# Quarter products that accumulate in shared PSUM tiles, a bias add moved to GpSimd, and a new bank split at the end of attention

## The chip, the cores and the metric

The kernel runs on one core of a Trainium2 chip. The metric is device time in microseconds (us), lower is better. The time before is 655.55 us, the median of three runs (655.39 to 655.63). One more execution was taken with the hardware profiler; all durations below are from that one.

## The reference

One decoder layer over x (2 batches x 512 tokens x 1024) and a context (2 x 1024 x 1024), all in float32:

```python
x = x + attention(layernorm(x), w_qkv, b_qkv, w_o, b_o)     # 32 heads of 32, 8 key/value heads, RoPE, causal
x = x + fake_quant(layernorm(x)) @ fake_quant(ctx)          # 512x1024 @ 1024x1024 for each batch
x = x + ffn(layernorm(x))                                   # below
# fake_quant(v) = (clip(round(v / s + z), 0, 255) - z) * s
# ffn(x): base  = x @ W_org.T
#         coeff = softmax((mean over tokens of x) @ Wq.T @ keys.T / sqrt(128))      # 8 experts
#         delta = sum over e of coeff[e] * (x @ down[e]) @ up[e]                     # rank 64 each
#         return base + delta
```

## The kernel before

**Stages.** Batch 0 and batch 1 are called 0 and 1. First come layer norm, the q, k and v products and the rotation. Then attention runs in 40 slots, followed by visits that only finish earlier slots. In the slots, PE also gets "fill": the second half of the k, q and v products, and batch 0's output product, context product and layer norms. After attention comes the tail: batch 1's output product ("wo"), batch 1's context product, the W_org product for both batches ("wb"), the low-rank "hidden" product, and the "up" product, which ends the kernel.

**An order written out by a planner.** The order of instructions on PE, DVE (VectorE), ACT (ScalarE) and Pool (GpSimd) is fixed when the program is built. `Clocks` estimates what each engine's clock would read after each instruction. Work off PE waits in `lanes` as `Hop`s; `dispatch` emits the head of a lane, in the sorted order of lane names, while its engine's estimated clock is at most `LEAD` (0.6 us) ahead of PE's, and `force(key)` emits lanes until that key is done. In the tail, units of PE work come from `g_post`, and at a `yield PAUSE` inside a long unit the small units whose inputs are ready (context tokens `C`, transposes `X`, column sums `cs`) are put between. Bulk loads are issued on SP's (SyncE's) queue; the bias row `bo`, the transposing DMAs of `mT` and `q1T` on ACT's.

**PSUM banks.** There are eight banks of 128x512, in two sets of four. `mm` takes a free bank among `allowed`, the one read longest ago. In attention a visit `i` computes scores into one set (`new`) and the transposed scores of slot `i - LAG` ("weights", L1218 and L1226) into the other (`old`). ACT turns weights into `pt` with an exponential (L1240), Pool masks `pt`'s diagonal blocks (L1245), `attend` multiplies `pt` by the values (L1267), and `evacuate` copies the result into `oT`. After each visit `allowed` is the set that fill may use, and the sets change roles (`filler`).

**Products by quarters.** Five products (wo of batch 1, wb of both batches, hidden, up) use Winograd's form of Strassen's scheme (`by_quarters`). Each matrix is cut in quarters, and seven products of quarter size take the place of eight:

```
P1 = A11 B11     P2 = A12 B21     P3 = S4 B22     P4 = A22 T4
P5 = S1 T1       P6 = S2 T2       P7 = S3 T3
C11 = P1 + P2                     C12 = P1 + P6 + P5 + P3
C21 = P1 + P6 + P7 + P4           C22 = P1 + P6 + P5 + P7
```

S and T are sums of quarters that DVE makes: `left_sums` and the tiles `s_`; `right_sums`, whose four groups are the keys ("to", 0) to ("to", 3) for wo, "tb" for wb, "td" for hidden and "tu" for up. The code counts quarters from 0, so that C12 is `(0, 1)`. In the row products each quarter product fills two banks with four matmuls each, in the up product four banks with two each; a matmul of two float32 operands is two instructions in the profile. Every product takes banks of its own. DVE adds a finished bank into the rows of `x` (`add`, L1795 and L1866) or into `hs` (L1835); hidden's first add of a quarter is a scaled copy on ACT. P1 is also copied by ACT into an SBUF tile `more` (L1724); DVE then adds P6 and later P7 into it (`gather`, L1711), and `more` goes into the quarters of C. The order is 2, 1, 5, 6, 3, 7, 4, in the up product 2, 1, 5, 6, 7, 3, 4. For wo of batch 1, P2 is computed while attention ends (`beside`).

**The other parts that the change touches.** `bias_lane` adds b_o to the four row tiles of x (128x1024 each) on DVE (L1046). `load_ctx` quantises the context in eight chunks; in the tail Pool sums their columns one chunk after another into `q2sum` (L1382), and `g_columns` turns that into column totals on PE with a matrix of ones (L1390). `quantize_rows` makes the bf16 rows `a1` and issues their transposing DMA (L1510), which sets the key ("A", b, t).

Of the kernel before, what the change touches and what calls it, by code (L numbers as in the profile page):

```python
# [111 lines left out]
class Clocks:  # L112
# [45 lines left out]
    def add(self, ins):  # L158
# [34 lines left out]
        elif engine == "PE":  # L193
            wide = "float32" in str(ins_[0].dtype)
            passes = 1 if not wide else 2 if ins.is_transpose else 4
            size = tuple(ins.tile_size) if ins.tile_size else (128, 128)
            if size != self.tile_size:
                start = max([start] + self.groups) + 0.2
                self.tile_size = size
            whole = size[0] * size[1] == 16384  # L200
            part = range(4) if whole else [max(ins.tile_position) // 32]
            done = max([start] + [self.groups[i] for i in part]) + max(n * passes / 2400.0, 0.055)
            for i in part:
                self.groups[i] = done
            self.at[engine] = done if whole else start + 0.015
            end = done + 0.2
        else:
            many = max([n] + [_free(a) for a in ins_])
            if kind in self.FIXED:
                us = self.FIXED[kind]  # L210
            elif many <= 16:
                us = self.SMALL
            elif engine == "Activation":
                scaled = len(ins_) > 1 and len(outs) == 1
                us = 0.15 + 0.00084 * many + 0.12 * (len(outs) > 1 or scaled and many > 900)
            elif engine == "Pool":
                us = 0.25 + 0.0008 * many
            elif kind == "CustomDveAnt":
                us = 0.08 + 0.00104 * many
            elif kind == "TensorScalarPtr" and len(ins_) < 2 + 2 and not ins.is_scalar_tensor_tensor:  # L220
                us = 0.12 + 0.00058 * many
            else:
                us = 0.08 + 0.00106 * many
                if kind == "TensorScalarPtr":
                    us += 0.05
                elif kind == "TensorTensor" and self.at["Pool"] > start and not _in_psum(ins_):
                    us += 0.1
            if kind == "TensorTensor" and engine == "Pool" and many <= 16:
                us = 0.45
            self.at[engine] = start + us  # L230
            end = start + us + 0.08
# [15 lines left out]
def kernel(  # L247
# [142 lines left out]
    taken = {}  # L390

# [34 lines left out]
    def mm(shape, name, dtype=F32):  # L426

        clocks.catch_up()
        could = [p for p in allowed if is_free(p)]
# [69 lines left out]
    LEAD = 0.6  # L499
    LEADS = {"Activation": 5.0, "Pool": 5.0}  # L500
# [117 lines left out]
    def fill(us):  # L618

        credit[0] += us  # L620
        while any_may() and (is_open() or credit[0] > UNIT / 2):
            if not step():
                credit[0] = min(credit[0], UNIT)
                break
# [420 lines left out]
    def add_bo(xi, bo_sb):  # L1045
        nc.vector.tensor_tensor(xi, xi, bo_sb, ALU.add)  # L1046

    def bias_lane(b, x_tiles, load):
# [16 lines left out]
        for t in range(NT):  # L1065
            lane(
                (4, "bias"),
                Hop("DVE", lambda t=t: add(t), lambda t=t: [got[0], x_tiles[t]], key=("bias", b, t), us=1.2),
# [206 lines left out]
    def attended_to(g, pv):  # L1275

        b, c = divmod(g, NC)
        if b not in oT:
            oT[b] = act.tile([P, NC, S], F32, tag="act", name=f"oT{b}")
        evacuate(oT[b][:, c, :], pv)  # L1280
# [6 lines left out]
    def load_ctx(b, bufs, dst, release):  # L1287
# [72 lines left out]
        if free[0]:  # L1360
            for k in range(1, CTX // P):
                mine = [("q2", b, i) for i, (n_, _) in enumerate(parts) if n_ in (k - 1, k)]
                last = {"key": ("q2sum", b), "made": lambda: [q2sum[b]]} if k == CTX // P - 1 else {}
# [20 lines left out]
    def g_columns(b):  # L1384
        corr[b] = const.tile([P, D], F32, tag="corr", name=f"corr{b}")
        for h in range(2):
            cols = slice(h * 512, (h + 1) * 512)
            ps = mm([P, 512], f"cs{b}_{h}")
            if b in q2sum:
                nc.tensor.matmul(ps, onesh, q2sum[b][:, cols], start=True, stop=True)  # L1390
# [303 lines left out]
    def by_quarters(product, a_, b_, s_, t_, more, add, hooks=(), late_third=False, ps2=None):  # L1694
# [8 lines left out]
        banks = range(len(more))  # L1703

        def add_all(i, j, srcs, first=False):
            for h in banks:
                add(i, j, h, srcs[h], first)

        def gather(ps):
            for h in banks:  # L1710
                nc.vector.tensor_tensor(more[h], more[h], ps[h], ALU.add)  # L1711

        if ps2:
            add_all(0, 0, ps2, True)
            then(0)
        else:
            then(0)
            ps = yield from product(2, a_(0, 1), b_(1, 0))
            add_all(0, 0, ps, True)
        then(2)  # L1720
        yield PAUSE
        ps = yield from product(1, a_(0, 0), b_(0, 0))
        for h in banks:
            nc.scalar.copy(more[h], ps[h])  # L1724
        add_all(0, 0, ps)
        then(1)
        yield PAUSE
        ps = yield from product(5, s_[0], t_(1))
        minus_(s_[0], a_(0, 1), s_[1])
        add_all(0, 1, ps, True)  # L1730
        add_all(1, 1, ps, True)
        then(5)
        yield PAUSE
        ps = yield from product(6, s_[1], t_(2))
        if len(s_) == 2:
            minus_(s_[1], a_(0, 0), a_(1, 0))
        gather(ps)
        add_all(0, 1, more)
        then(6)
        yield PAUSE  # L1740

        def third():
            ps = yield from product(3, s_[0], b_(1, 1))
            add_all(0, 1, ps)
            then(3)
            yield PAUSE

        def seventh():
            ps = yield from product(7, s_[-1], b_(0, 1))
            gather(ps)  # L1750
            add_all(1, 1, more)
            add_all(1, 0, more, True)
            then(7)
            yield PAUSE

        for p in (seventh, third) if late_third else (third, seventh):
            yield from p()
        ps = yield from product(4, a_(1, 1), t_(4))
        add_all(1, 0, ps)
        then(4)  # L1760

    def left_sums(s_, a_):
        nc.vector.tensor_tensor(s_[0], a_(1, 0), a_(1, 1), ALU.add)
        minus_(s_[1], s_[0], a_(0, 0))
        if len(s_) == 3:
            minus_(s_[2], a_(0, 0), a_(1, 0))

    def rows_product(name, b, pauses=True):
        def product(p, l, r):
            n = NK // 2  # L1770
            ps = [mm([P, 512], f"{name}{p}_{b}_{i}") for i in range(2)]
            for i in range(2):
                for k in range(n):
                    nc.tensor.matmul(  # L1774
                        ps[i], l[:, k, i * P : (i + 1) * P], r(k), start=(k == 0), stop=(k == n - 1)
                    )
                    yield 0.86
                if not i and pauses:
# [5 lines left out]
    def rows_by_quarters(name, b, lhs, weight, t_, hooks, ps2=None):  # L1784
# [13 lines left out]
        more = tail["more"]([P, 2, 512], f"more{name}{b}")  # L1798
        if not ps2:
            hooks[0] = [lambda: left_sums(s_, a_)] + hooks.get(0, [])  # L1800
        yield from by_quarters(product, a_, b_, s_, t_, [more[:, i, :] for i in range(2)], add, hooks, ps2=ps2)
# [3 lines left out]
    def store(b, t, cols):  # L1805
        i = b * NT + t
        nc.sync.dma_start(out[i * P : (i + 1) * P, cols], xs[b][t][:, cols])

    def hidden_by_quarters():
# [7 lines left out]
        def product(p, l, r):  # L1817
            ps = [mm([P, S], f"h{p}_{i}") for i in range(2)]
            for i in range(2):
                for k in range(n):  # L1820
                    nc.tensor.matmul(  # L1821
                        ps[i], r(k)[:, i * P : (i + 1) * P], l[:, k, :], start=(k == 0), stop=(k == n - 1)
                    )
                    yield 0.86
            return ps
# [12 lines left out]
        s_ = [act.tile([P, n, S], F32, tag="half", name=f"sh{i}") for i in range(2)]  # L1838
        more = tail["more"]([P, 2, S], "moreh")
        left_sums(s_, a_)  # L1840
# [3 lines left out]
        yield from by_quarters(product, a_, b_, s_, t_, [more[:, i, :] for i in range(2)], add)  # L1844

    def up_by_quarters():
# [6 lines left out]
        def product(p, l, r):  # L1853
            ps = [mm([P, 512], f"up{p}_{t}") for t in tiles]
            for t in tiles:
                for k in range(n):
                    nc.tensor.matmul(  # L1857
                        ps[t], l[:, k, t * P : (t + 1) * P], r(k), start=(k == 0), stop=(k == n - 1)
                    )
                    yield 0.86  # L1860
            return ps
# [9 lines left out]
        parts = {(0, 0): 2, (0, 1): 3, (1, 0): 2, (1, 1): 2}  # L1871
# [3 lines left out]
        more = [tail["q2"]([P, 2, S], f"moreu{i}") for i in range(2)]  # L1875
        more = [m[:, i, :] for m in more for i in range(2)]

        def sums_left():
            left_sums(s_, a_)

        def sums_right():
# [3 lines left out]

        yield from by_quarters(
            product, a_, b_, s_, t_, more, add, {0: [sums_right], 2: [sums_left]}, True
        )

    def chain_units(b, w_keys):  # L1890

        turned = [("q", n) for n in range(B * NC)] + [("k", n, h) for n in range(B) for h in range(2)]
        columns = [("q2sum", b)] if b else [("q2", b, i) for i in range(CTX // P)]
# [146 lines left out]
    def visit(i):  # L2040
# [29 lines left out]
        for s in range(4):  # L2070
            if s == 1 and g >= 0:
                empty([(new, 0)])
                pv = take_bank((new, 0))
# [16 lines left out]
        filler[0] = new  # L2090
        last_slots = i + 1 >= n_slots
        allowed[:] = [(1 - new if last_slots else new, s) for s in range(4)]
# [57 lines left out]

    def output_left(i):
        s_ = [sums["S"][:, j, :, :] for j in range(2)]
        a_ = lambda i, j: oT[1][:, (1 - j) * half : (2 - j) * half, i * 256 : (i + 1) * 256]
        if i:
# [4 lines left out]
    def sums_lane(makers, name, sources):  # L2159

        for i, fns in enumerate(makers):
            for k, fn in enumerate(fns):
                key = {"key": (name, i)} if k == len(fns) - 1 else {}
                lane((1 if name == "to" else 2, name), Hop("DVE", fn, lambda k=k: sources(k), **key))
# [5 lines left out]
    )  # L2170
    sums_lane(wo_makers, "to", lambda k: ())
# [26 lines left out]
    def output_by_quarters():  # L2198
# [3 lines left out]
            2: [lambda: force(("S1",)), lambda: force(("to", 0))],  # L2202
            5: [lambda: force(("to", 1))],
            3: [lambda: rows_quantised(0), lambda: force(("to", 2)), lambda: org_rows(0)],
# [5 lines left out]
    def base_unit(b):  # L2210
        hooks = {}
        if b == 0:
# [5 lines left out]
                1: [lambda: force(("tb", 0))],  # L2218
                5: [lambda: force(("tb", 1))],
                3: [lambda: force(("tb", 2))],  # L2220
                7: [lambda: force(("tb", 3))],
            }
        yield from rows_by_quarters("wb", b, x3T[b], lambda k: org[k], org_sums[0], hooks)
# [94 lines left out]
```

## Time and profile before

| | us |
|---|---|
| median of the three runs | 655.55 |
| the profiled execution's own time | 655.19 |
| its span, first to last instruction | 653.5 |
| PE busy | 631.9 (97%) |
| DVE busy | 514.5 (79%) |
| ACT busy | 299.6 (46%) |
| Pool busy | 128.8 (20%) |
| granted TensorE clock, mean | 0.999 |

The span is what a profile's rows cover, and 1.7 us of the execution's time lie outside it. PE is busy almost throughout, so most rows of the profile describe work beside PE's. Rows of the timeline have the start, the duration, the engine, the line, the operation, what it writes and reads, shapes and a count, and in brackets the idle time of the engine before it with what ended that. Rows of the list of waits have the waiting engine and line, who released it, the total, the number and the longest. PEld is PE's weight load; an engine's name with a q is its queue, SPq for example.

### The profile page before, as it was taken

The numbers are of one execution on the slowest core, as the hardware profiler recorded it, in microseconds if no ns is written. First come the engines' busy times: TensorE is split into PE (matmuls) and PEld (weight loads), VectorE is DVE, ScalarE is ACT, GpSimd is POOL, SyncE is SP. The second block draws the span as 40 slices with busy tenths as digits, with TensorE's granted clock in tenths as the row PEclk, the third lists the DMA queues.
The fourth block names the chain that finished last, engine by engine and source line by source line (L and its number), as shares of the span: only waits on it lengthen the run. The fifth ranks groups of instructions, "written<-read, shape, count | busy, mean of one in ns | idle before, by whom it ended". The sixth has DMA issues, their size and how long they took to land. (4 is left out here: it accounts for less than half of the span.)

```text
span 653.5 us, 9247 instructions
## 1 busy us (share of the span) xinstructions
PE 631.9 (97%) x3190; PEld 301.6 (46%) x3190; DVE 514.5 (79%) x1187; ACT 299.6 (46%) x808; POOL 128.8 (20%) x253
## 2 busy tenths in 40 slices
PE   5998999999999999999999999999999999999997
PEld 5753344444444444444444444444345544444443
DVE  5799889888778988888887689998998544553685
ACT  2145576686655768888897433554101100110100
POOL 2100133233313232333233320440110000000000
PEclk9999999999999999999999999999999999999999
DMA  9930000002021230120101146591000002000105
GB/s 290 335 83 2 9 9 10 10 1 73 10 73 65 73 106 10 46 101 34 33 2 25 25 134 237 169 314 32 1 1 0 33 31 97 1 0 1 65 0 193
DMA packets 42478, 44.64 MB, mean 68 GB/s; under 512 B 19264, under 2 KB 32576, under 8 KB 42432
## 3 DMA queue, kind: packets, MB, share of 16 engines
q1 hardware_dynamic: 24992, 38.82, 17.4%
q10 hardware_dynamic: 17440, 5.25, 4.2%
q8 instruction: 25, 0.41, 0.2%
q14 instruction: 21, 0.17, 0.1%
HBM read 35.66 MB, written 4.19 MB: 61 GB/s over the span
## 5 line engine op out<-in xcount | busy, mean ns | idle before, releaser
L1147 ACT ACTIVATE ms<-ms,stats 128x512 f32<-128x512 f32 (+3 forms) x256 | 141.0, 558 | 70.1 <-DVE stats L1132 70.1
L1132 DVE CUSTOM_DVE_ANT_0 ms<-bank,mask 128x512 f32<-128x512 f32 (+3 forms) x256 | 108.5, 487 | 14.7 <-PE bank L1120 12.9
L1240 ACT ACTIVATE pt<-bank 128x512 f32<-128x512 f32 x160 | 88.0, 590 | 25.3 <-PE bank L1267 9.0
L751 PE MATMUL bank<-xT,wq 128*128 128x512 f32 x192 | 88.0, 600 | 2.7 <-DVE stats L1132 2.7
L1245 POOL TENSOR_SCALAR_AFFINE_SELECT pt<-pt 128x512 f32<-128x512 f32 x64 | 48.9, 782 | 94.5 <-ACT pt L1240 90.3
L1411 PE MATMUL bank<-wo,oT 128*128 128x512 f32 x128 | 59.1, 604 | 0.7 <-ACT pt L1240 0.7
L751 PEld LDWEIGHTS bank<-xT,wq 128*128 128x128 f32 x192 | 34.7, 190 | 41.3 <-issue 35.7
L1218 PE MATMUL bank<-qT,kT 32*128 32x128 f32 (+3 forms) x512 | 49.3, 439 | 1.3 <-DVE x L1420 0.6
L1147 ACT ACTIVATION_READ_ACCUMULATOR ms<-ms,stats 128x1 f32 x256 | 50.1, 196 | 0.0
L1120 PE MATMUL bank<-kT,qT 32*128 32x128 f32 (+3 forms) x512 | 49.0, 461 | 0.0
L1120 PEld LDWEIGHTS bank<-kT,qT 32*128 32x128 f32 x512 | 24.2, 183 | 34.9 <-ACT pt L1240 10.5
L1267 PE MATMUL bank<-pt,v 128*32 128x128 f32 (+3 forms) x512 | 37.8, 435 | 0.0
L1411 PEld LDWEIGHTS bank<-wo,oT 128*128 128x128 f32 x128 | 23.1, 189 | 26.8 <-issue 24.2
L1193 POOL TENSOR_TENSOR stats<-stats,log 128x16 f32<-128x16 f32 x16 | 6.5, 409 | 142.7 <-ACT log L1184 100.3
L1218 PEld LDWEIGHTS bank<-qT,kT 32*128 32x128 f32 x512 | 25.6, 185 | 14.6 <-issue 7.8
L1795 DVE TENSOR_TENSOR x<-x,bank 128x512 f32<-128x512 f32 x36 | 23.1, 680 | 11.1 <-PE bank L1774 5.7
L1411 PE MATMUL bank<-q,q1T 128*128 128x512 bf16 x128 | 28.6, 379 | 1.6 <-ACT pt L1240 1.6
L1267 PEld LDWEIGHTS bank<-pt,v 128*32 128x32 f32 x512 | 16.4, 109 | 27.7 <-issue 24.8
L1774 PE MATMUL bank<-worg,S 128*128 128x512 f32 x64 | 28.3, 592 | 0.0
L1774 PE MATMUL bank<-worg,x3T 128*128 128x512 f32 x64 | 28.0, 594 | 0.0
L1774 PE MATMUL bank<-tb,S 128*128 128x512 f32 x64 | 27.9, 593 | 0.0
L743 DVE TENSOR_TENSOR qT<-bank,qT 128x512 f32<-128x512 f32 x28 | 18.9, 686 | 9.6 <-PE bank L751 9.5
(226 smaller groups left out, 1021.4 us busy)
## 6 DMA issues: line engine op xcount, KB each, us to landing
wq<-in_wqT_dram SPq DMA_DIRECT2D x8, 512.0 KB, 8.5
ctx_raw<-in_ctx_dram SPq DMA_DIRECT2D x8, 512.0 KB, 3.2
wo<-in_woT_dram SPq DMA_DIRECT2D x8, 512.0 KB, 3.1
raw<-in_ctx_dram SPq DMA_DIRECT2D x8, 512.0 KB, 3.9
worg<-in_worgT_dram SPq DMA_DIRECT2D x8, 512.0 KB, 6.2
out_dram<-x SPq DMA_DIRECT2D x16, 256.0 KB, 2.1
x<-in_x_dram SPq DMA_DIRECT2D x7, 512.0 KB, 6.7
x_raw<-in_x_dram SPq DMA_DIRECT2D x4, 512.0 KB, 7.4
```

What stands on the lines that cost most here:

```text
L743: nc.vector.tensor_tensor(dst, ps, other, ALU.add)
L751: nc.tensor.matmul(ps[:, part], weight[:, k, :], xs_[:, k, part], start=(k == 0), stop=(k == n - 1),)
L1120: nc.tensor.matmul(sc[s][:, part], qTs[b, c][row(s), t * P : (t + 1) * P], kTs[b][row(s), c // 4, : (t + 1) * P], start=True, stop=True,)
L1132: nc.vector.tensor_tensor_reduce(out=of[s][:, part], in0=sc[s][:, part], in1=mask[:, S - (t + 1) * P :], scale=-scale, scalar=BIG, op0=ALU ...
L1147: nc.scalar.activation(ms[:, part], ms[:, part], AF.Exp, bias=stats[g][:, t, s, 0:1], scale=-1.0, accum_out=stats[g][:, t, s, 1:2],)
L1218: nc.tensor.matmul(sc[s][:, part], kTs[b][row(s), c // 4, kb * P : (kb + 1) * P], qTs[b, c][row(s), kb * P :], start=True, stop=False,)
L1240: nc.scalar.activation(pt[:, s, :], sc[s][:, :n], AF.Exp, scale=scale)
L1245: nc.gpsimd.affine_select(out=diagonal, in_=diagonal, compare_op=ALU.is_ge, fill=0.0, base=0, pattern=[[0, 4], [1, P]], channel_multiplier=-1,
L1267: nc.tensor.matmul(pv[row(s), kb * P :], vs[b][:, kb, h * HD : (h + 1) * HD], pt[:, s, part], start=(kb == 0), stop=(kb == NT - 1),)
L1411: nc.tensor.matmul(ps, l[:, t * P : (t + 1) * P], r[:, cols], start=(k == 0), stop=(k == many - 1))
L1774: nc.tensor.matmul(ps[i], l[:, k, i * P : (i + 1) * P], r(k), start=(k == 0), stop=(k == n - 1))
L1795: nc.vector.tensor_tensor(xh, xh, src, ALU.add)
```

## The change

The change has these parts.

- `by_quarters`: P1, P6, P5 and P3 accumulate one after the other in the same banks, P7 and P4 in two (four) others. After each product DVE (ACT, where hidden's add is the first) adds the bank as it stands into one quarter of C, right behind the half that filled it. `more`, its ACT copies and `gather` are gone. The order is 2, 1, 6, 5, 3, 7, 4; in hidden 1, 6, 5, 2, 3, 7, 4. `held` keeps a chain's banks from `mm` until its last product.
- S4 gets a tile of its own in the row and up products, and hidden's first S is made behind P7 of wb 1. The hooks that force sums move to match; "to" 0 and 1 are now needed for the second product in the chain. The lanes of tb are sorted ahead of the row lanes.
- The bias of batch 1 is added on Pool, and `Clocks` prices Pool's two-input operation higher.
- `q2sum` leaves out the last chunk, which `g_columns` adds with one more matmul for each half.
- Just before the last copy into `oT`, the transposing DMA of batch 0's last row tile is forced out.
- From visit `n_slots` on the bank sets no longer change roles, and the value product takes its bank with `mm`.
- When fill finds no unit that may start, `dispatch` looks ahead by IDLE = 2.5 us.

The diff, cut to its core:

```diff
@@ Clocks.add
-                us = 0.25 + 0.0008 * many
+                us = 0.1 + 0.0021 * many if kind == "TensorTensor" else 0.25 + 0.0008 * many
@@ mm
-        could = [p for p in allowed if is_free(p)]
+        could = [p for p in allowed if is_free(p) and p not in held]
@@ fill
             if not step():
                 credit[0] = min(credit[0], UNIT)
+                dispatch(IDLE)
                 break
@@ add_bo
-        nc.vector.tensor_tensor(xi, xi, bo_sb, ALU.add)
+        (nc.gpsimd if free[0] else nc.vector).tensor_tensor(xi, xi, bo_sb, ALU.add)
@@ bias_lane
-                Hop("DVE", lambda t=t: add(t), lambda t=t: [got[0], x_tiles[t]], key=("bias", b, t), us=1.2),
+                Hop(
+                    "Pool" if b else "DVE",
...
@@ attended_to
+        if g == last - 1:
+            force(("A", 0, NT - 1))
         evacuate(oT[b][:, c, :], pv)
@@ load_ctx
-            for k in range(1, CTX // P):
+            for k in range(1, CTX // P - 1):
...
@@ g_columns
-                nc.tensor.matmul(ps, onesh, q2sum[b][:, cols], start=True, stop=True)
+                nc.tensor.matmul(ps, onesh, q2sum[b][:, cols], start=True, stop=False)
+                yield 0.22
+                nc.tensor.matmul(
+                    ps, onesb, q2_of(b, CTX // P - 1)[:, cols], start=False, stop=True
+                )
@@ by_quarters
-    def by_quarters(product, a_, b_, s_, t_, more, add, hooks=(), late_third=False, ps2=None):
+    def by_quarters(product, a_, b_, s_, t_, add, hooks=(), ps2=None, order="21653"):
...
+        where = {1: (0, 0), 2: (0, 0), 6: (1, 0), 5: (1, 1), 3: (0, 1), 7: (1, 1), 4: (1, 0)}
+        seen = set()
+
+        def summed(n):
+            first = where[n] not in seen
+            seen.add(where[n])
+            return lambda h, ps: add(*where[n], h, ps, first)
...
+        chains = {}
+        for n in map(int, order + "74"):
+            chain = 2 if n == 2 else 7 if n in (7, 4) else 1
+            ps = yield from product(n, *factors[n](), chains.get(chain), summed(n))
+            if chain not in chains:
+                chains[chain] = ps
+                if chain != 2:
+                    held.update(of_name[p.name] for p in ps)
+            if n in (3, 4):
+                held.difference_update(of_name[p.name] for p in ps)
+            then(n)
+            if n != 4:
+                yield PAUSE
@@ rows_product (hidden's and up's product likewise)
-        def product(p, l, r):
+        def product(p, l, r, on=None, each=lambda *_: None):
             n = NK // 2
-            ps = [mm([P, 512], f"{name}{p}_{b}_{i}") for i in range(2)]
+            ps = on or [mm([P, 512], f"{name}{p}_{b}_{i}") for i in range(2)]
             for i in range(2):
                 for k in range(n):
                     nc.tensor.matmul(
...
+                        start=(k == 0 and not on),
+                        stop=(k == n - 1),
+                        skip_group_check=on is not None,
                     )
                     yield 0.86
+                each(i, ps[i])
@@ visit
             if s == 1 and g >= 0:
-                empty([(new, 0)])
-                pv = take_bank((new, 0))
+                pv = take_bank((new, 0)) if i < n_slots else mm([P, S], f"pv{g}")
                 attend(g, pv)
...
-        filler[0] = new
-        last_slots = i + 1 >= n_slots
-        allowed[:] = [(1 - new if last_slots else new, s) for s in range(4)]
+        if i < n_slots:
+            filler[0] = new
+        allowed[:] = [(1 - new if i + 1 == n_slots else new, s) for s in range(4)]
@@ output_by_quarters
-            2: [lambda: force(("S1",)), lambda: force(("to", 0))],
-            5: [lambda: force(("to", 1))],
-            3: [lambda: rows_quantised(0), lambda: force(("to", 2)), lambda: org_rows(0)],
+            1: [lambda: force(("S1",)), lambda: force(("to", 1))],
+            6: [lambda: force(("S4",))],
+            5: [lambda: force(("to", 2))],
+            3: [lambda: rows_quantised(0), lambda: org_rows(0)],
@@ base_unit
+        else:
+            hooks = {7: [hidden_first_sum]}
```

## The prediction

> **What bounds the kernel now.** I read the page first (busy time, the 40 slices), then busy time by windows of 20 and 40 us, the list of who waited for whom on PE, and the timeline from 355 us on.
>
> ```profile
> PE 631.9 (97%) x3190; PEld 301.6 (46%) x3190; DVE 514.5 (79%) x1187; ACT 299.6 (46%) x808; POOL 128.8 (20%) x253
> PE   5998999999999999999999999999999999999997
> DVE  5799889888778988888887689998998544553685
> POOL 2100133233313232333233320440110000000000
> ```
>
> PE is busy for 97% of the span: 21.6 us of 653.5 are idle. The windows say where:
>
> ```profile
> 0.00:20.00 20.00, 12.50 (x93) 11.82 (x94) 11.28 (x27) 4.37 (x8) 4.95 (x18) 1.00 0.94 310
> ...
> 340.00:380.00 40.00, 36.93 (x286) 17.32 (x285) 29.78 (x72) 25.57 (x68) 14.01 (x31) 1.00 0.10 20
> ...
> 460.00:480.00 20.00, 18.74 (x65) 8.11 (x64) 19.40 (x30) 2.42 (x3) 2.12 (x1) 1.00 0.01 1
> ...
> 640.00:653.50 13.50, 9.18 (x22) 3.80 (x20) 6.12 (x10) 0.00 (x0) 0.00 (x0) 0.96 0.44 166
> ```
>
> The first figure after each length is PE's. Idle are 7.5 us at the start and 4.3 us after the last matmul, both out of this change's reach; 3.07 us between 340 and 380; 1.26 us between 460 and 480. From 380 to 649 nothing else is missing, so DVE work saved there buys nothing by itself. The two holes have names:
>
> ```profile
> PE bank L1411 <- ACT pt L1240: 2.3, 3, 0.9
> PE bank L1390 <- POOL q2sum L1382: 1.3, 1, 1.3
> PE bank L473 <- ACT pt L1240: 0.8, 1, 0.8
> ```
>
> **Attention's end.** The last visits (L2090 to L2092). Before, the weights and the fill behind them use the same four banks, so fill waits until an exponential has read one. After, from visit n_slots on, weights keep one set and fill and the value product have the other.
>
> ```profile
> 358.01 1.89 PE L1411 MATMUL bank<-q,q1T 128*128 128x512 bf16 x8 [0.71 <-ACT pt L1240]
> 360.79 1.89 PE L1411 MATMUL bank<-q,q1T 128*128 128x512 bf16 x8 [0.89 <-ACT pt L1240]
> 362.60 0.71 PE L1218 MATMUL bank<-qT,kT 32*128 32x256 f32 x8
> ...
> 364.64 3.70 PE L1411 MATMUL bank<-wo,oT 128*128 128x512 f32 x8 [0.67 <-ACT pt L1240]
> ...
> 378.51 1.14 PE L473 MATMUL bank<-ident,xn_c 128*128 128x128 f32 x8 [0.80 <-ACT pt L1240]
> ```
>
> All four waits go: 0.71 + 0.89 + 0.67 + 0.80 = 3.07 us. What is late next: the weights at 362.60 now need the set that the exponentials of the visit before still read; ACT ends them at 360.14 + 1.57 = 361.71. Without the first two waits PE would be there at 361.0; it starts at about 361.8, so only 0.8 of that 1.6 us is kept. The other two are kept whole: 0.8 + 0.67 + 0.80 = 2.25 us. The later value product waits for GpSimd's mask, over at 382.17 against PE's 383.11; that chain moves forward by 1.5 us, PE by 2.25, which just fits. Bounds: 0 (other waits take their place) to 3.07. The longer look-ahead of lanes (IDLE, where fill finds no unit) only reorders DVE work; I price it at nothing, because fill runs dry nowhere but here: 0.9 us of PE idle from 220 to 340 is all it could win, and a DVE item of 1.2 us put ahead of a bank read is what it could cost.
>
> **The column sums.** At L1390 PE waits for q2sum. The eighth chunk leaves the GpSimd sum and becomes a second matmul per half. The final ACT write ends at 465.37, the GpSimd add behind it ran 2.13 us, and PE stood 1.26 us. Without the add the chunk is there a microsecond before PE asks: -1.26. Added: two matmuls. L1390's two took 0.59 us, 0.30 each; L1411's bf16 ones 1.89/8 = 0.24. Cost 0.5 to 0.6 us; I take 0.5, PE-bound, so all of it counts.
>
> **Work removed.** It buys only slack. For each pair of banks, 9 adds x 2 plus 2 gathers x 2 become 7 x 2: 8 DVE instructions fewer of 0.60 us start to start (four in 2.47), 4.8 us in each of three row products, and 16 x 0.60 = 9.6 us in the up product. The twelve ACT copies of product 1 go as well. Four bias adds of 1.22 us leave DVE. All of it lay beside PE work.
>
> **The added wait** is PE on DVE. A product's second use of a bank must wait until DVE has read the first. Before, each product took fresh banks among eight. A half product is eight instructions, 3.43 us in the chain of waits; the add starts up to 0.2 us after its bank's end and takes 0.68. So DVE may run 2.5 us late before PE stops, and with PE stop all its followers, the small C and X units too. How late was DVE? Product 6 ended at 414.74, its gather began at 416.23 (1.5 us); product 7, 1.6 us; the next part's product 2, 2.0 us; and in one place 4.6 us (a product from 449.08 ends at 455.9, at 16 x 0.43):
>
> ```profile
> 452.75 1.28 DVE L1795 TENSOR_TENSOR x<-x,bank 128x512 f32<-128x512 f32 x2 [2.47 <-ACT morewb L1724]
> ...
> 460.50 2.47 DVE L1795 TENSOR_TENSOR x<-x,bank 128x512 f32<-128x512 f32 x4
> ```
>
> That lateness began with DVE waiting 2.47 us for the ACT copy that is removed, and after the change adds stand right behind their own half. Bounds: 0 to 2.1 us (4.6 - 2.5) there, as much again in the part before. I take 0.6 in all, nearer to the rows that fit. In hidden and up the first three products' reads sit on ACT, idle there, or have three other banks of time; DVE was busy for 28.5 of the 60 us from 540 to 600. Hidden's product 6 comes second now and needs one sum of 2.3 us and eight of 0.34 (1.43 for four): 5 us under product 1's 6.9. Nothing; were that cover gone, 5 us.
>
> **Bias on GpSimd**, and the earlier product 6. GpSimd's 128x1024 two-input add took 2.12 us, so four are 8.5 us on a queue that was idle for 14.9 us before 398. They fall where DVE makes the right-hand sums, and there the trace shows a price:
>
> ```profile
> 426.83 2.12 POOL L1382 TENSOR_TENSOR q2sum<-q2sum,q 128x1024 f16<-128x1024 f16 x1
> ...
> 427.40 1.57 DVE L1440 TENSOR_TENSOR off_b<-off_b,qp_sb 128x1 f32<-128x1 f32 x1
> ...
> 399.72 0.69 DVE L644 TENSOR_TENSOR to<-wo,to 128x512 f32<-128x512 f32 x1
> ...
> 400.13 3.60 PE L1774 MATMUL bank<-to,S 128*128 128x512 f32 x8
> ```
>
> A 128x1 add that takes 0.16 us elsewhere lasted until GpSimd's ended at 428.95. S at 436.15 took 2.28 us for 1.22 the same way, and one add from SBUF 1.42 for 0.68; adds from PSUM kept 0.68. Over the six q2sum adds from 409 to 441 DVE lost 1.41 + 1.06 + 0.74 = 3.2 us, 0.54 each; four biases would lose 2.1. The bounds from these rows are 0, and 8.5 if every bias is waited out whole as in L1440's. [...]
>
> It matters because product 6 now runs right after product 1, at the 400.13 where product 5 started, and needs to 1, whose last piece began at 399.72. Its fourth slice is needed 3 x 0.86 = 2.6 us after the start, at 402.7; the piece is done at 400.4: 2.3 us to spare. A loss of 2.1 fits: 0. At 8.5 the stall is 6.2 us. I take 0, nearest to the measured losses, and keep 6.2 for the range. The biases also tie x between the two engines: a DVE add on a tile whose bias runs waits up to 2.1 us, which lies within those 6.2.
>
> **Edits at nothing.** The forced transpose of the last row tile: it is issued at 382.76 already, ahead of the copy at 385.61. Loads: the diff moves none; the bulk ones are on SP's queue now, and bo stays on ACT's. Here the change does nothing that its title says, at no cost.
>
> **The sum**, against the profiled execution (655.19 us; span 653.5, 1.7 around it; the median of the runs is 655.55, 0.36 more): -2.25 - 1.26 + 0.5 + 0.6 + 0 = -2.4 us. From the median: 653.1.
>
> **Rivals.** *No change*: the gains of attention come back as waits of the value product for GpSimd's mask, or DVE loses five of the 8.5 us to GpSimd, so that PE stands 2.7 us at product 6. For it: DVE is 98% busy from 400 to 440, so lateness there is not made good. Against: 14 us of DVE work leave this stretch. Price: -2.4 + 2.7 = +0.3, 655.8; with the former, 655.2.
> [...]
> *More*: all 3.07 us and no lateness: -3.07 - 1.26 + 0.5 = -3.8, 651.7; with the 0.9 from 220 to 340, 650.8.
>
> **How the numbers follow.** About 0.2% (1.3 us) is what a measurement of this kernel can tell from no change. Forecast and its better variant 0.62 (own range 650.8 to 654.2); no change 0.22; slower 0.16. The range goes from 650.8 to 656.8 and leaves out most of the slower case and a sliver below.
>
> **What would show it.** Right: no wait of L1411 or L473 on pt after 355 us, and of the weights on pt at most 1 us; no wait on q2sum; four GpSimd bias adds between 390 and 402; PE idle from 380 to 640 below 1 us; part order 2, 1, 6, 5, 3, 7, 4. [...]

## The result and the profile after

The changed kernel took 662.01 us (661.59 to 662.79), the kernel before 655.63 us on the same chip: ratio 1.0097 [1.0083, 1.0112], 6.4 us slower. The forecast was 653.1, with 656.8 as the upper end of its range. The profiled execution took 662.79 us, its span is 661.1.

First the page of after, busy time and three rows of the 40 slices:

```profile
PE 637.2 (96%) x3192; PEld 304.7 (46%) x3192; DVE 486.9 (74%) x1136; ACT 292.6 (44%) x795; POOL 134.0 (20%) x256
...
PE   5998999999999999999999997999999999999997
...
DVE  5799888898778988888787778579895633432743
...
POOL 2000133333212233323233333331100000000000
```

DVE lost 28 us of work, as meant, and it bought nothing. PE has a new 7 in the slice from 397 to 413 us. The list of who waited for whom on PE names it:

```profile
PE bank L474 <- DVE xn_c L466: 4.3, 1, 4.3
...
PE bank L1771 <- DVE x L1798: 1.2, 2, 1.0
PE bank L1403 <- ACT q L1338: 1.0, 1, 1.0
```

The waits on pt that the prediction wanted to be rid of are gone, and of the one on q2sum 0.13 us are left. What stands in their place is a wait of the transposes of row tile 3 (L474) for the normalised rows xn_c. The chain of waits of after, cut to 384 to 403 us (start, length, what), leads from there back to a load:

```profile
384.52 7.46 DMA bo<-in_bo_dram
...
392.20 4.68 POOL x L1049 x2
...
396.91 0.69 DVE x L1798
397.59 1.21 DVE st_c L457 x2
...
399.30 0.56 POOL rstd_c L462
...
399.88 2.83 DVE xn_c L466
...
402.85 1.30 PE bank L474 x5
```

The bias vector bo lands, GpSimd adds it to two row tiles, DVE can then add a bank to the second of these, takes the statistics, GpSimd takes the power that gives 1/sigma, and DVE normalises. The timeline (start, length; in brackets the idle time and its releaser) shows what each step cost:

```profile
392.20 6.98 POOL L1049 TENSOR_TENSOR x<-x,bo 128x1024 f32<-128x1024 f32 x3 [10.46 <-DMA bo<-in_bo_dram]
...
394.59 0.69 DVE L1798 TENSOR_TENSOR x<-x,bank 128x512 f32<-128x512 f32 x1 [1.86 <-POOL x L1049]
...
396.91 0.69 DVE L1798 TENSOR_TENSOR x<-x,bank 128x512 f32<-128x512 f32 x1 [1.63 <-POOL x L1049]
...
399.82 2.34 POOL L1049 TENSOR_TENSOR x<-x,bo 128x1024 f32<-128x1024 f32 x1
399.88 2.82 DVE L466 TENSOR_SCALAR xn_c<-x,mv_c,rstd_c 128x1024 f32<-128x1024 f32 x1
...
402.85 1.94 PE L474 MATMUL bank<-ident,xn_c 128*128 128x128 f32 x8 [4.35 <-DVE xn_c L466]
...
404.58 4.05 PE L1771 MATMUL bank<-to,S 128*128 128x512 f32 x5
```

DVE stood 1.86 and 1.63 us, each time because the x tile that it had to add to was in GpSimd's hands. At 399.82 the fourth bias began, 0.06 us before xn_c, and xn_c took 2.82 us for its usual 0.81: it ended 0.54 us after GpSimd let go. Then the last lines: eight transposes in 1.94 us, which take 1.04 to 1.14 elsewhere in this stretch, and matmuls of 0.85 us start to start, which take 0.43. Windows of 2 us from 398 on show why (the first figure after the length is PE's busy time, the first after POOL's brackets the granted clock):

```profile
398.00:400.00 2.00, 0.51 (x2) 0.00 (x0) 1.86 (x6) 1.01 (x1) 1.88 (x3) 1.00 1.05 390
400.00:402.00 2.00, 0.00 (x0) 0.00 (x0) 2.00 (x1) 0.23 (x1) 2.00 (x1) 0.81 0.63 231
402.00:404.00 2.00, 1.15 (x6) 1.18 (x7) 2.00 (x4) 0.03 (x1) 0.15 (x1) 0.50 0.01 5
404.00:406.00 2.00, 2.00 (x6) 1.26 (x5) 2.00 (x4) 1.15 (x2) 0.00 (x0) 0.50 0.00 0
406.00:408.00 2.00, 2.00 (x4) 0.68 (x3) 2.00 (x4) 0.00 (x0) 0.00 (x0) 0.50 0.00 0
408.00:410.00 2.00, 2.00 (x6) 0.99 (x5) 0.76 (x3) 0.00 (x0) 0.00 (x0) 0.98 0.00 0
```

After 4.35 us of idleness PE worked at a granted clock of 0.50 for some 5 us, which costs about 2.6 us more. The 0.81 of the window from 400 to 402 says that the clock had fallen at about 401.2, while PE still stood.

**The ledger.** From attention's last scores to hidden's first matmul the two traces differ by 6.9 us (204.2 and 211.1). I charge each matmul with the time until the next one starts and sort the differences by the matmuls' operands:

| part | predicted | after |
|---|---|---|
| attention's end (mT, q1T and qT matmuls) | -2.25 | -2.5 |
| column sums, with the wait ahead of them | -0.76 | +0.4 |
| row products waiting for DVE to read a bank | +0.6 | +2.0 |
| start of the output product: stall and half clock | 0 | +7.0 |
| sum | -2.4 | +6.9 |

Before the last scores after is 0.8 us later, and the same kernel code there differs by as much between profiles; from hidden on the two differ by 0.1 us in all. The profiled execution of after was the slowest of its five, so that the ledger's sum is a little above the 6.4 us between the medians.

### The profile page after: what moved, and what is told of

Its sections match the earlier page's. It is cut to its first block, busy times and chain, and to the rows that moved or that the text cites. A ratio compares the mean times of both kernels' runs of the same rounds, so it can differ in the third digit from the quotient of the medians.

```text
span 661.1 us, 9163 instructions
## 1 busy us (share of the span) xinstructions
PE 637.2 (96%) x3192; PEld 304.7 (46%) x3192; DVE 486.9 (74%) x1136; ACT 292.6 (44%) x795; POOL 134.0 (20%) x256
## 4 chain that ended last, share of the span: by engine, by line
PE 84%; DVE 8%; issue 2%; DMA 2%; POOL 1%; ACT 1%; ACTq 0%; SPq 0%; DVEq 0%; POOLq 0%
PE bank L754 22%; PE bank L1771 15%; PE bank L1426 11%; PE bank L1882 7%; PE bank L1835 7%; PE bank L1129 6%; PE bank L1227 5%; PE bank L1276 5%; PE bank L474 2%; PE bank L1235 1%; DVE tb L647 1%; DVE ms L1141 1%; DMA bo<-in_bo_dram 1%; POOL x L1049 1%; DVE x L1798 1%
## 5 line engine op out<-in xcount | busy, mean ns | idle before, releaser
L1798 DVE TENSOR_TENSOR x<-x,bank 128x512 f32<-128x512 f32 x42 | 28.7, 684 | 47.3 <-PE bank L1771 43.7
L1897 DVE TENSOR_TENSOR x<-x,bank 128x512 f32<-128x512 f32 x28 | 18.8, 688 | 19.8 <-PE bank L1882 19.8
L1853 ACT ACTIVATE hs<-bank,coef 128x512 f32<-128x512 f32 x8 | 5.5, 687 | 57.9 <-PE bank L1835 57.9
```

## The experiments

My theory: the bias on GpSimd makes the loss, by its place in two queues and by the blocking, and the half clock multiplies it. Rivals: the new order of the products (2, 1, 6) makes the loss by itself, without GpSimd; or the new bank split does. A third question is what the forced transpose, priced at nothing, was worth.

**Bias back on DVE (e1), and its opposite (e2).**

```diff
 e1 = after with
-(nc.gpsimd if free[0] else nc.vector).tensor_tensor(xi, xi, bo_sb, ALU.add)
+nc.vector.tensor_tensor(xi, xi, bo_sb, ALU.add)
-"Pool" if b else "DVE",
+"DVE",
 e2 = before with these lines the other way round, and the new price in Clocks.add
```

> The changed kernel with the four bias adds of batch 1 back on DVE, all else kept. Theory (the bias queue on GpSimd holds row tile 3's norm, PE stands 4.35 us in front of its transposes and then runs some 5 us at half clock): both go, 4.35 + 2.6 us less than 662.0, so 654.5 to 655.5 us, PE idle between 390 and 412 us under 0.5. Rival (product 6 comes too early for its right-hand sums, so that DVE is late whoever adds the bias): PE still waits 3 us or more in that stretch, 659 or more.

> The kernel before with only the bias of batch 1 moved to GpSimd, and the planner's price of its adds with it; products in banks of their own, old order. Theory: the same chain exists here (bias row's landing, GpSimd, DVE add on the same x tile, row tile 3's norm, transposes), only that a half of product 5 stands ahead of the transposes: 3.4 us more cover than in the changed kernel, so a stall of 1 to 2.5 us and a time of 656 to 659. Rival (accumulation is at fault): 655.0 to 656.0, no wait of the transposes on xn_c.

e1: ratio 0.9975 [0.9964, 0.9986], 1.6 us faster than before (the medians, 655.07 and 656.19, are 1.1 apart). The wait on xn_c is gone and the clock stays at 1.00; of the three new waits in PE's list two are left:

```profile
PE bank L1403 <- ACT q L1338: 1.0, 1, 1.0
...
PE bank L1771 <- DVE x L1798: 0.8, 2, 0.5
```

e2: 1.0018 [1.0007, 1.0028], 1.2 us slower than before. PE's list has these two new lines:

```profile
PE bank L1774 <- DVE tb L644: 0.9, 1, 0.9
...
PE bank L473 <- DVE xn_c L465: 0.6, 1, 0.6
```

So one edit costs 1.0097 - 0.9975, about 8 us, in the new kernel and 1.2 in the old. In e2 half of product 5 stands between product 1 and the transposes, and it covers most of it: xn_c was normalised at 403.65, later than in after, yet PE waited 0.6 us for it. The order of the products alone is not the cause, as e1 keeps 2, 1, 6 and loses nothing there.

The edit also changed where the planner put the transposes. In e1 half of product 6 stands ahead of them; in after they come right behind product 1. These are rows of e1:

```profile
396.71 0.81 DVE L466 TENSOR_SCALAR xn_c<-x,mv_c,rstd_c 128x1024 f32<-128x1024 f32 x1
...
398.39 3.60 PE L1771 MATMUL bank<-to,S 128*128 128x512 f32 x8
...
401.83 1.04 PE L474 MATMUL bank<-ident,xn_c 128*128 128x128 f32 x8
```

The place by itself explains little of the stall. In after DVE began the last three of the four sums that product 6 needs at 402.63, behind xn_c. My estimate from this row is that product 6, put first, would have stood nearly as long for its second slice; no run tried it.

**The same adds at other places (e3, e9).**

```diff
 e3 = after with the biases in another order
-for t in range(NT):
+for t in (2, 3, 0, 1) if b else range(NT):
-if t == NT - 1:
+if t == (1 if b else NT - 1):
     give_xn()
 e9 = after with the biases emitted behind the transposes of row tile 3
+can=(lambda: ("X", 0, NT - 1) in done) if b else None,
```

> The changed kernel with GpSimd's biases in the order of tiles 2, 3, 0, 1, so that product 2's and product 1's adds into tiles 0 and 1 stand ahead of the biases of those tiles and DVE doesn't wait for them. If the wait of DVE on x is what makes row tile 3 late, PE's 4.35 us stall falls to under 2 us and with it the half clock: 656 to 659. If the queue on GpSimd and its exclusion of DVE are enough (the power step still stands behind two biases), a stall of 3 us or more stays: 660 to 662.5.

> The changed kernel with the bias still on GpSimd, but no bias add emitted before row tile 3 of batch 0 is turned on PE. If only the place in the queue was at fault (ahead of that tile's norm), the 4.35 us stall and the half clock go and the time is that of e1_bias_on_dve or a little less, 654 to 655.5. If GpSimd's adds beside DVE's sums cost time wherever they stand (exclusion, and the tie on x), PE then waits for DVE at products 6 and 5: 656.5 to 659.

e3: 1.0008 [0.9996, 1.002]; the wait on xn_c is 2.02 us where it was 4.35. DVE's two waits for x tiles, 1.86 and 1.63 us, are gone, so they were a part of it. In their place the power step stands behind two biases in GpSimd's queue (DVE idles 1.56 us for it), and the blocking stays, as three rows of its timeline show:

```profile
397.38 0.55 POOL L462 TENSOR_TENSOR rstd_c<-rstd_c,power 128x1 f32<-128x1 f32 x1
...
397.90 5.12 POOL L1049 TENSOR_TENSOR x<-x,bo 128x1024 f32<-128x1024 f32 x2
397.96 2.83 DVE L466 TENSOR_SCALAR xn_c<-x,mv_c,rstd_c 128x1024 f32<-128x1024 f32 x1 [1.56 <-POOL rstd_c L462]
```

e9: 1.0114 [1.0099, 1.0128]. The edit moves an add in the order in which instructions are emitted, but GpSimd runs ahead of PE: the first bias still ran beside xn_c, at 396.03, and xn_c took 2.96 us. PE didn't wait for that, since half of product 6 now stood ahead of the transposes. With the other three adds later, the sums for the next products are what GpSimd blocks:

```profile
406.43 6.18 DVE L647 TENSOR_TENSOR to<-wo,to 128x512 f32<-128x512 f32 x3
...
406.59 5.48 POOL L1049 TENSOR_TENSOR x<-x,bo 128x1024 f32<-128x1024 f32 x2 [2.43 <-DVE x L1799]
...
415.01 1.22 PE L1772 MATMUL bank<-to,S 128*128 128x512 f32 x1 [4.74 <-DVE x L1799]
```

Three sums that take 1.89 us in e1 took 6.18, and PE waited 4.74 us for a DVE add that came at the end of that. At each of the three places tried (after, e3, e9) the biases on GpSimd cost PE a stall; that another place would be free is not ruled out.

**Is the half clock a cost of its own (e4)?** Five useless 128x512 matmuls, 4.46 us in the trace, are put into the bank of the transposes ahead of them, so that PE isn't idle while it waits.

```diff
+if name == "c0_3" and g == 0:
...
+    for _ in range(5):
+        nc.tensor.matmul(ps..., wo[0][:, :P], oT[1][:, 0, :], start=True, stop=True)
...
```

> The changed kernel with five useless 512-column matmuls (4.3 us of PE work) into the bank that the late transposes then overwrite, so that PE works through its 4.35 us wait; nothing else moves. If the halved clock after the stall comes from the idle time, matmuls behind it take 0.43 us again instead of 0.85 and the time falls by 2 to 2.6 us, to 659.4 to 660. If the slow matmuls have another cause (late operands), it stays at 661.5 to 662.5.

1.0054 [1.0036, 1.0071]: more work, and about 2.8 us less time than after (1.0097). The window from 400 to 420 of e4 has a granted clock of 1.00, where after has 0.83:

```profile
400.00:420.00 20.00, 19.40 (x52) 8.81 (x51) 16.52 (x22) 5.05 (x6) 4.32 (x2) 1.00 0.19 65
```

So of the loss some 4.4 us are the stall and some 2.6 the clock behind it. The lengths of the waits draw no line here: 2.02 us in e3 were followed by a clock of 0.54 from 402 to 404, 2.71 us in e8 (below) by 0.54 from 478 to 480, 2.30 us in e10 by 1.00 from 464 to 472. Two windows of e3:

```profile
402.00:404.00 2.00, 1.82 (x4) 0.42 (x3) 2.00 (x2) 0.68 (x2) 1.01 (x1) 0.54 0.03 10
404.00:406.00 2.00, 2.00 (x4) 0.73 (x4) 2.00 (x5) 0.00 (x0) 0.00 (x0) 0.61 0.00 0
```

The length of the wait alone does not decide it. In after the clock fell at 401.25, 2.7 us into the wait (the windows from 401.00 to 401.25 and from 401.25 to 401.50 give 1.00 and 0.50), and was back at 408.07 (0.50 from 407.80 to 408.07, 0.99 from 408.07 to 408.30). In e3 the 0.54 and 0.61 put the fall at about 402.2, when PE had been working again for 1.2 us, and the return at about 405.6, if the clock stood at 0.50 in between as in after. So it was low for 6.8 us in after and for some 3.4 in e3. Why the wait of e10 had no fall behind it these runs don't show.

**The end of attention (e6, e7, e8).** e6 is e1 with the old bank roles, e7 is before with the new ones, e8 is e7 with the new price of GpSimd's adds.

```diff
 e7 = before with
+pv = take_bank((new, 0)) if i < n_slots else mm([P, S], f"pv{g}")
+if i < n_slots:
+    filler[0] = new
+allowed[:] = [(1 - new if i + 1 == n_slots else new, s) for s in range(4)]
 e6 = e1 with these lines as in before; e8 = e7 with, in Clocks.add,
+us = 0.1 + 0.0021 * many if kind == "TensorTensor" else 0.25 + 0.0008 * many
```

> The changed kernel with the bias on DVE (as in e1_bias_on_dve) and with the end of attention as it was before (sets change roles, value product in the new set). If the new bank split is worth what was forecast, 2.25 us (2.4 by the traces), this is 2.2 to 2.6 us slower than e1_bias_on_dve, and the four waits on pt are back with 3.1 us in all. If the split is worth nothing, both are equal.

> The kernel before with the new bank split at the end of attention alone. The same question from the other side: 2.2 to 2.6 us under the kernel before, ratio about 0.9963. And it says what accumulation and the column sums are worth: if this is faster than e1_bias_on_dve (0.9975), accumulating in PSUM and the second matmul cost time rather than save it; by the traces they cost 1.2 us of waits on DVE and 0.4 us.

> e7_before_new_end with the planner's price of GpSimd's two-input operation raised from 1.07 to 2.25 us for 1024 columns (the trace has 2.12), which puts the column sums one half product later and changes no arithmetic. If PE's 1.3 us wait at the column sums came from that price, it goes and this is 1.2 to 1.4 us under e7_before_new_end, some 652 us; a candidate for the fastest version. If the last chunk's chain is simply late, the wait stays.

e6: 1.0019 [1.0005, 1.0032]; the waits of before on pt, 2.3 and 0.8 us, are back, so the split is worth 0.0044 of 655.6, 2.9 us, in the new kernel. In the old kernel it went the other way: e7 1.0181 [1.0163, 1.0199], e8 1.0095 [1.0082, 1.0109]. PE's list of e7 begins, behind the start's, with

```profile
PE bank L1390 <- POOL q2sum L1382: 6.1, 1, 6.1
PE bank L1411 <- DMA q1T<-a_b: 4.4, 1, 4.4
```

I had not foreseen the second of these. The transposing DMA for the last row tile was issued at 384.05 in e7, and at 384.15 SP sent off the first of four bulk loads of x, which the earlier end of attention had released. The transpose landed after 8.8 us. In before it was issued at 382.76 and the x loads at 385.65: 3.1 us. The price in e8 cut the wait on q2sum to 2.7 us and left the one on q1T.

**The forced transpose (e10, e11, e13).**

```diff
 e10 = e7 with (e11 = e8 with); e13 = e1 without
+if g == last - 1:
+    force(("A", 0, NT - 1))
 evacuate(oT[b][:, c, :], pv)
```

> The kernel before with two parts of the change alone: the new bank split at the end of attention and the forced transposing DMA (e7_before_new_end with the latter). In e7 the transposing DMA was issued 0.1 us before the bulk loads of x and PE waited 4.39 us for it, then ran at half clock. If that order against the bulk loads is the cause, the wait goes and the time is 2.2 to 2.6 us under the kernel before, about 653.2: the fastest so far, and accumulation with the second matmul then costs about 1.5 us. If the new split delays the transposing DMA in another way, the wait stays at 2 us or more.

> e10 with the planner's price of GpSimd's two-input operation at 2.25 us for 1024 columns, so that the column sums stand half a product later on PE. If the price is what makes PE wait there, the wait of 1.3 us goes: 651.7 to 652.2. If the sums are late for another reason, no gain.

> The changed kernel with the bias on DVE (e1) and without the forced transposing DMA, so that the last copy into oT stands ahead of it on ACT. If its order against the bulk loads matters, PE waits about 4.4 us for q1T and then runs some 5 us at half clock: 6 to 7 us over e1, about 661.5. By the prediction's price, nothing: equal to e1.

e10: 0.9968 [0.9953, 0.9983]; e11: 0.997 [0.9956, 0.9984]; e13: 1.0077 [1.0058, 1.0096]. Two lines turn e7 into a kernel faster than before, and taking them out of e1 costs 0.0102 of 656.5, 6.7 us. In e10 q1T landed after 4.8 us, and of e7's 6.1 us on q2sum 2.3 are left; in e13 q1T landed after 8.6, and e13's list of waits has

```profile
PE bank L1424 <- DMA q1T<-a_b: 4.6, 1, 4.6
```

So the transposing DMA ahead of the bulk loads is a condition of the bank split. The two lines also put the last copy into `oT` on DVE, where e7 and e13 have it on ACT ahead of the DMA; what holds the DMA up among the loads no view shows. The price of GpSimd's adds added nothing to it.

**The column sums later (e12).** In e1 the planner puts the sums up before the last chunk is there. A likely cause is in `Clocks`: it prices the issue of a transposing DMA at 0.1 us of ACT's time, and in the trace the issue takes 1.25 us, just ahead of the write of the chunk (the first and third rows below). e12 holds them back by 1.5 us.

```diff
 e12 = e1 with, in ready():
+late = 1.5 if key == ("q2", 1, CTX // P - 1) else 0.0
-return key in done and done[key] <= clocks.now("PE") + 0.1 - margin[0]
+return key in done and done[key] + late <= clocks.now("PE") + 0.1 - margin[0]
```

> The changed kernel with the bias on DVE (e1) and the column sums of batch 1 held back until 1.5 us after the planner's time for the last chunk. In e1 PE stands 0.97 us between the q2sum matmul and the one of the last chunk. If that is a chunk that arrives a microsecond later than planned, the wait goes and this is 1.0 to 1.3 us under e1. If the chain behind the sums (rows, context product, norms) has no slack, the time comes back later as another wait.

0.9944 [0.9928, 0.9961]: 653.18 us for 656.45, the fastest kernel here and faster than both given ones. In the timelines, e1 first, then e12:

```profile
465.12 1.25 ACTq L1525 DMA_TRANSPOSE q1T<-a_b  x1
...
466.27 0.38 PE L1401 MATMUL bank<-q2sum,onesh 128*128 128x512 f16 x1
...
466.42 1.15 ACT L1338 ACTIVATE q<-raw,minus 128x1024 bf16<-128x1024 f32 x1 [1.33 <-issue]
...
467.62 0.38 PE L1403 MATMUL bank<-q,onesb 128*128 128x512 bf16 x1 [0.97 <-ACT q L1338]
...
468.26 2.31 PE L1771 MATMUL bank<-worg,morewb 128*128 128x512 f32 x5
```

```profile
468.38 0.38 PE L1402 MATMUL bank<-q2sum,onesh 128*128 128x512 f16 x1
...
468.60 0.38 PE L1404 MATMUL bank<-q,onesb 128*128 128x512 bf16 x1
...
469.25 2.31 PE L1772 MATMUL bank<-worg,S 128*128 128x512 f32 x5
```

The sums take 1.99 us in e1 (468.26 - 466.27) and 0.87 in e12. The ratios of e1 and e12 are 2.0 us apart, their traces 1.6 from the last scores to hidden. Of this 1.1 us are the sums and 0.3 a short wait for q2sum ahead of them; the rest is open.

## Where the prediction was right and wrong

**Bias on GpSimd** is the step that failed, 0 taken and 7.0 measured; it alone turns the sign. Three things in it went wrong.
- The price was taken as the mean loss over the q2sum adds (0.54 us each). The mean hid how long a single block can be: xn_c lost 2.0 us in one piece, beside a GpSimd add of 2.34 us. The operation that makes xn_c has one SBUF tensor as input and took 2.82 us for 0.81 in after, 2.83 in e3 and 2.96 in e9.
- I costed the victim that the diff names ("to" for product 6) and not the one that stands in front of it. The x adds, through which DVE gets to the statistics of row tile 3, wait for the tiles that GpSimd is adding to. I had written that x is tied between the engines and counted this inside the 6.2 us of "to". It is a chain of its own: 1.86 + 1.63 us of waiting for x and 2.0 of blocking make DVE 5.5 us late, of which 4.35 reached PE. GpSimd's queue itself cost nothing in after, where the third bias ended at 399.18 and the power step's input came at 399.22; in e3 it cost 1.56 us. The slower case, a stall of 6.2 us ahead of product 6, had the sign, the place and the blocking right. PE stood 4.35 us and not 6.2, for the transposes, which after has ahead of product 6; the sums "to" were late behind them, at 402.63.
- Nothing was set aside for the clock, though the trace of before had rows for it: PE's first work, after 7.26 us of waiting, in the timeline of before:

```profile
7.26 1.97 PE L473 MATMUL bank<-ident,xn_a 128*128 128x128 f32 x8 [7.26 <-DVE xn_a L465]
9.06 1.94 PE L751 MATMUL bank<-xT,wk 128*128 128x128 f32 x8
10.84 1.06 PE L751 MATMUL bank<-xT,wv 128*128 128x128 f32 x8
```

Eight matmuls of one shape take 1.97 and 1.94 us until 10.84, and 1.06 from there on: 3.6 us at half speed behind a long wait, 1.8 us lost. (The trace's clock records begin at 10.73, so the 1.00 that the windows give before that isn't a reading; the durations tell it.)

**Column sums**: -0.76 predicted, +0.4 measured. The wait for q2sum went down to 0.13 us, and a new one on the last chunk (0.96 us in after, 0.97 in e1) took its place, since the planner saw the chunk as ready too early. e12 takes it away, and its ledger gives -1.0 for the part.

**Added wait**: +0.6 taken, +2.0 measured in after and 1.5 in e1, within the bounds of 0 to 4.2. It falls in wb of batch 0: at the first half of product 6, whose bank product 1 had filled and where DVE runs a pair of sums of 1.29 us ahead of the bank's read (0.98 us in after, 0.52 in e1), at the first half of product 5 (0.26), and by tenths at other halves.

**Attention's end**: -2.25 predicted, -2.5 measured in after; by e6 it is 2.9. The four waits went, and the weights, which start at 361.61 in after, took 0.9 us longer than in before, about what the prediction had taken off for them. **Forced transpose**: "at no cost" held for before's timing only. With the bank split the bulk loads follow the transpose by 0.1 us, or by 0.6 where it is forced, instead of 2.9, and the two lines are worth 6.7 us. That the change moves no loads was wrong: the earlier end of attention moved those of x. The sum of the prediction was right here because both edits were made; the reason was wrong. **Work removed**, **hidden and up**: nothing, as said. The look-ahead by IDLE was not tried alone. Two slips in the working change nothing in the forecast: the 0.9 us of idle PE lie between 180 and 340, with 0.6 from 220 on, and the first form of "no change" adds up to 655.4, not 655.2.

Without the bias on GpSimd the other parts give 655.07 us (e1), and with the sums held back 653.18 (e12). The latter looks near the forecast of 653.1, but that is partly luck: the kernel before stood at 656.45 beside it, so 3.3 us were gained where 2.4 were forecast, and the terms are not those of the sum. The added wait is larger, and the sums' gain needed another edit.

## What to carry to other kernels

When work moves to another engine, list what stands behind it on that engine's queue and who shares its buffers, and follow each to PE; price a block by the longest single instruction, not by a mean (here 2.0 us for xn_c, where the mean was 0.54). A stall on a busy PE can cost more than its length: the 4.35 us in after cost about 2.6 more through the clock. An edit that ends a stage earlier can also start the next stage's loads earlier, as in e7, where q1T then landed after 8.8 us instead of 3.1: look which small urgent transfer they now run beside.

## What the runs showed of the hardware

- A DMA transpose landed after 3.1 us with bulk loads 2.9 us behind it (before), after 4.7 and 4.9 with them 0.6 us behind (after, e1), and after 8.6 and 8.8 with them 0.1 us behind (e13, e7). The load of bo took 5.3 us in before, where it was issued 1.6 us ahead of the x loads, and 7.5 in after and 8.5 in e1, 0.7 us behind them.
- A 128x1024 fp32 DVE operation with one SBUF tensor and two scalars took 2.82 us in after, 2.83 in e3 and 2.96 in e9 beside a GpSimd add, and 0.81 in e1. It ended 0.54 us behind the add in after and 0.55 in e9, where its row starts 0.06 us ahead of the add's; DVE adds that read a bank kept their 0.69 us beside the adds in after.
- The granted clock fell to 0.50 in after, 2.7 us into a wait of 4.35 us, and stayed there for 6.8 us. In e3 it was 0.54 and 0.61 in two windows of 2 us behind a wait of 2.02 us, in e8 0.54 behind one of 2.71, and in e10 1.00 behind one of 2.30. At the start of before, after 7.26 us of waiting, two groups of eight matmuls took 1.97 and 1.94 us, and such groups 1.06 from 10.84 on.
- In after, e1 and e12 ACT stood 1.33 us ahead of its write of the last chunk, and the issue of a transposing DMA filled 1.25 of them.
